# A new order for TensorE's steps in a slot of a fused attention kernel, with an aligned program stream

## Chip, cores and metric

The kernel runs on one core of one Trainium2 chip. The metric is device time in microseconds (us), the median of the runs; the kernel before takes 3887.73 us (3 runs, 3886.52 to 3889.18).

## What is computed

Input: 8 sequences of 512 tokens with 128 features, all in float32. An attention layer with a Taylor-series kernel comes first, then six layers of windowed attention with a feed-forward each, both wrapped in layer norms:

```python
x = x + _layernorm(_L0_attn_ref(_layernorm(x), ...))     # once, about the first 530 us
x = x + _layernorm(_L0_ffn_ref(_layernorm(x), ...))

def _L0_ffn_ref(x, ...):
    for i in range(DEPTH):                               # 6 layers
        x = attn_layer(shift_tokens(x), Wqkv[i], q_scale[i], k_scale[i], Wo[i]) + x
        x = ffn_layer(shift_tokens(x), ...) + x

def attn_layer(x, Wqkv, qs, ksc, Wo):                    # 16 heads of 64
    q, k, v = split(x @ Wqkv)
    q = l2norm(q) * qs ; k = l2norm(k) * ksc             # then rotary tables on q and k
    out = local_attention(q, k, v)                       # windows of 32, each sees itself and the one before
    return out @ Wo

def ffn_layer(x, ...):                                   # 128 -> 2 x 341 -> 128
    a, gate = split(layer_norm(x) @ W1 + b1)
    return a * gelu(gate) @ W2 + b2
```

## The kernel before

The change bears on the six layers. A *unit* is one block of 128 tokens of one sequence in one layer: 6 layers x 8 sequences x 4 blocks = 192 units. The main loop (L703) runs over *slots* t. In each slot TensorE does a different step for each of several units, so that the other engines have time between two steps of the same unit (`at(t, lag, step)` runs a step on unit t - lag):

- unit t: `proj` 0 and 1 (q and k, L421), `values` (v, L481), `unit_length` (the scaling of q and k);
- unit t-1: `by_features` 0 and 4 (transposes of q and k, four head pairs each, L511), `scores` (the mask L527, the scores L534, then maximum, exponentials and their sums);
- unit t-2: `by_keys` (transposes of the exponentials, L562), `weigh_values` (L574, the tile po), `out_by_features` (transposes of the result, L594);
- unit t-3: `out_project` (L603, the tile py, added to the state by VectorE at L608).

After the last block of a sequence the feed-forward follows, spread over slots: `feed_norm` with lag 3, `feed_first` 4, `feed_middle` 5 (gelu), `feed_last` 6. Each of these falls on one slot of four, so each slot has one of them.

TensorE's order is written out by hand (`tc.manual_schedule`, L694). The order of the instructions on VectorE, ScalarE and GpSimd is chosen by the framework's scheduler, from the order of the code, priorities (`tc.high_priority`) and extra edges that the kernel adds with `issue_behind`. SyncE issues the transfers, among them eight for each unit that spread v over the windows (L489 to L492).

The order of TensorE's steps in a slot is: q (`proj` 0), output projection, k (`proj` 1), transposes of exponentials, v (`values`), transposes of q and k (first half), po (`weigh_values`), transposes of q and k (second half), feed-forward step, mask and scores (tile sp), transposes of the result.

PSUM is divided into rings by tag. "mm" has two buffers of two banks: q, k, v and the feed-forward's products take turns. "tr" has two buffers of one bank: all transposes and py. "s" has one buffer of two banks: po and sp take turns. A step that takes a buffer waits until the readers of its last content are done.

What each product leaves for the other engines: q and k are read by VectorE (L429 twice, L436: the rotation) and by ScalarE (L444 twice: squares); their sums of squares are made at L457. v is copied by ScalarE (L482). Transposes are copied by ScalarE (L514 for q and k, L564 for the exponentials, L596 for the result). sp is read by the maximum (L542, VectorE) and the exponentials (L546, ScalarE, 16 instructions). po is divided by the sums at L582 (VectorE). The feed-forward's layer norm (L99 to L117) reads its PSUM tile nx twice, for the statistics (L105) and for the normalisation (L115).

## Time and profile before

| | |
|---|---|
| median of 3 runs | 3887.73 us |
| the profiled execution | 3893.85 us |
| its span (first to last instruction) | 3892.1 us |
| granted TensorE clock over the span | 0.99 |
| busy: TensorE, VectorE, ScalarE, GpSimd | 3729.8, 2818.2, 2657.5, 1837.0 us |
| TensorE's instructions | 65600 matmuls and as many weight loads |
| mean busy share of the DMA engines, 600 us to the end | 0.25 to 0.27 in each stretch |

The profile names an instruction by engine, line, operation and what it writes and reads: `sp<-kT,qT` is a matmul into the tile sp. PE is TensorE, PEld its weight loads, DVE VectorE, ACT ScalarE, POOL GpSimd. A float32 product shows as two matmuls for each one in the code. In a list of groups the numbers behind the bar are busy time, mean duration of one (ns) and the idle time of the engine just before; behind `<-` stands what ended it. In the list of waits a row gives who waited for whom, the total in us, how often, and the longest. "issue" is idle time with no releaser in the profile. In a timeline a row gives start, duration, engine and what ran; idle time before it stands in brackets. A matmul's end is modelled and reaches beyond the start of the next, so idle time between matmuls is a lower bound.

### The profile page before, as it was taken

The numbers are of one execution on the slowest core, as the hardware profiler recorded it, in microseconds if no ns is written. First come the engines' busy times: TensorE is split into PE (matmuls) and PEld (weight loads), VectorE is DVE, ScalarE is ACT, GpSimd is POOL, SyncE is SP. The second block draws the span as 40 slices with busy tenths as digits, with TensorE's granted clock in tenths as the row PEclk, the third lists the DMA queues.
The fourth block names the chain that finished last, engine by engine and source line by source line (L and its number), as shares of the span: only waits on it lengthen the run. The fifth ranks groups of instructions, "written<-read, shape, count | busy, mean of one in ns | idle before, by whom it ended". The sixth has DMA issues, their size and how long they took to land.

```text
span 3892.1 us, 149565 instructions
## 1 busy us (share of the span) xinstructions
PE 3729.8 (96%) x65600; PEld 2474.2 (64%) x65600; DVE 2818.2 (72%) x4300; ACT 2657.5 (68%) x6745; POOL 1837.0 (47%) x1311
## 2 busy tenths in 40 slices
PE   8999989999999999999999999999999999999997
PEld 4555456666666666666666666666666666666665
DVE  4555567777867777777777777777787777777775
ACT  5565656776767777777777677777677777766664
POOL 0000025555555555555555555555555555555552
PEclk9999999999999999999999999999999999999998
DMA  2000012222222222222222322223222222222221
GB/s 81 17 9 12 6 50 71 59 66 60 76 74 63 63 63 66 71 75 65 60 62 64 82 65 66 65 56 82 70 66 59 66 65 56 65 68 68 64 67 37
DMA packets 153208, 233.46 MB, mean 60 GB/s; under 512 B 32622, under 2 KB 53356, under 8 KB 151788
## 3 DMA queue, kind: packets, MB, share of 16 engines
q1 hardware_dynamic: 152556, 223.89, 22.4%
q8 instruction: 517, 8.47, 0.9%
q14 instruction: 135, 1.11, 0.1%
HBM read 24.54 MB, written 4.19 MB: 7 GB/s over the span
## 4 chain that ended last, share of the span: by engine, by line
PE 89%; ACT 5%; issue 3%; DVE 2%; DMA 0%; POOL 0%; POOLq 0%; DVEq 0%; SPq 0%; ACTq 0%
PE tr L70 17%; PE mm L421 17%; PE mm L481 9%; PE py L603 9%; PE sp L534 7%; PE po L574 6%; PE y L282 4%; PE mm L625 3%; PE py L657 3%; PE mm L626 3%; PE sc L252 2%; PE sp L527 2%; ACT sq L444 2%; PE vv L230 2%; PE po L318 2%
## 5 line engine op out<-in xcount | busy, mean ns | idle before, releaser
L454 POOL TENSOR_TENSOR qk<-t,t 128x1024 f32<-128x1024 f32 x384 | 909.2, 2368 | 999.6 <-DVE t L436 999.5
L421 PE MATMUL mm<-wqkv,state 128*128 128x512 f32 x1536 | 727.1, 596 | 3.7 <-ACT v L482 2.6
L470 POOL TENSOR_TENSOR qk<-qk,ss 128x1024 f32<-128x1024 f32 x384 | 722.3, 1902 | 16.0
L429 DVE TENSOR_TENSOR t<-mm,tab 128x512 f32<-128x512 f32 x768 | 497.8, 685 | 242.8 <-PE mm L421 231.3
L546 ACT ACTIVATE pe<-sp,mx 128x64 f32<-128x64 f32 x3072 | 651.4, 376 | 27.6 <-DVE mx L542 27.3
L436 DVE TENSOR_TENSOR t<-mm,tab 128x1024 f32<-128x1024 f32 x384 | 465.9, 1213 | 0.0
L457 DVE TENSOR_REDUCE ss<-sq 128x16 f32<-128x1024 f32 x384 | 461.9, 1203 | 2.0 <-ACT sq L444 2.0
L444 ACT ACTIVATE sq<-mm 128x512 f32<-128x512 f32 x768 | 422.6, 610 | 47.2 <-DVE t L436 45.6
L603 PEld LDWEIGHTS py<-oT,wo 128*128 128x128 f32 x3072 | 374.8, 193 | 93.5 <-issue 56.2
L70 PEld LDWEIGHTS tr<-ident,qk 128*128 128x128 f32 x3072 | 345.7, 141 | 127.1 <-issue 105.7
L70 PE MATMUL tr<-ident,qk 128*128 128x128 f32 x3072 | 412.1, 277 | 7.4 <-ACT qT L514 2.3
L596 ACT COPY oT<-tr 128x512 f32<-128x512 f32 x384 | 207.3, 589 | 266.2 <-PE tr L70 265.2
L421 PEld LDWEIGHTS mm<-wqkv,state 128*128 128x128 f32 x1536 | 264.1, 192 | 191.6 <-issue 188.0
L481 PE MATMUL mm<-wqkv,state 128*128 128x512 f32 x768 | 367.9, 602 | 16.8 <-ACT sq L444 16.8
L603 PE MATMUL py<-oT,wo 128*128 128x128 f32 x3072 | 376.0, 276 | 1.0 <-ACT oT L596 0.9
L582 DVE TENSOR_TENSOR on<-po,su 128x1024 f32<-128x1024 f32 x192 | 235.1, 1224 | 170.1 <-PE po L574 170.1
L534 PEld LDWEIGHTS sp<-kT,qT 64*32 64x32 f32 x24576 | 271.9, 106 | 116.7 <-issue 113.8
L574 PE MATMUL po<-v,pT 64*32 64x64 f32 x24576 | 299.3, 225 | 44.7 <-issue 44.7
L482 ACT COPY v<-mm 128x1024 f32<-128x1024 f32 x192 | 194.5, 1013 | 211.0 <-PE mm L481 211.0
L534 PE MATMUL sp<-kT,qT 64*32 64x64 f32 x24576 | 312.2, 227 | 26.0 <-issue 25.2
L574 PEld LDWEIGHTS po<-v,pT 64*32 64x32 f32 x24576 | 258.5, 105 | 86.4 <-issue 86.2
L542 DVE TENSOR_REDUCE mx<-sp 128x16 f32<-128x1024 f32 x192 | 234.6, 1222 | 106.9 <-PE sp L534 106.3
(108 smaller groups left out, 5171.0 us busy)
## 6 DMA issues: line engine op xcount, KB each, us to landing
v<-v SPq DMA_DIRECT2D x1152, 128.0 KB
v<-v SPq DMA_DIRECT2D x672, 64.0 KB
wqkv<-in_L_ffn_Wqkv_dram SPq DMA_DIRECT2D x6, 1536.0 KB
wo<-in_L_ffn_Wo_dram SPq DMA_DIRECT2D x6, 512.0 KB
xin<-_attn_hidden_states_dram SPq DMA_DIRECT2D x8, 256.0 KB
xr<-_attn_hidden_states_dram SPq DMA_DIRECT2D x8, 256.0 KB
x<-xr SPq DMA_DIRECT2D x8, 256.0 KB
xr<-x SPq DMA_DIRECT2D x8, 256.0 KB
```

The source lines that it names most:

```text
L70: nc.tensor.transpose(ps[:cols, :rows], src, ident[:rows, :rows])
L421: nc.tensor.matmul(ps[:, a].rearrange("p h d -> p (h d)"), lhs, wqkv[:, s, a, :], start=True, stop=True)
L429: nc.vector.tensor_tensor(t2[:, a], ps[:, 1 - a], tab[:, 2 * s + 1, j, HF * a : HF * (a + 1)].unsqueeze(1).to_broadcast([P, H, HF]), ALU.mult,
L436: nc.vector.tensor_tensor(t1, ps, tab[:, 2 * s, j, :].rearrange("p (a d) -> p a d", a=2).unsqueeze(2) .to_broadcast([P, 2, H, HF]), ALU.mult,)
L444: nc.scalar.activation(sq[:, :, a, :], ps[:, a], AF.Square)
L454: nc.gpsimd.tensor_tensor(qk[:, s].rearrange("p h a d -> p a h d"), t1, t2, ALU.add)
L470: nc.gpsimd.tensor_tensor(t, t, ss[:, i, :].unsqueeze(2).to_broadcast([P, H, HD]), ALU.mult)
L481: nc.tensor.matmul(ps[:, p, :], lhs, L["wqkv"][:, 2, p, :], start=True, stop=True)
L534: nc.tensor.matmul(sp[W * w : W * (w + 1), p, pair, :], qT[HD * p : HD * (p + 1), pair, W * w : W * (w + 1)], kT[HD * p : HD * (p + 1), pa ...
L546: ex = nc.scalar.activation(pe[:, pair, p, :], sp[:, p, pair, :], AF.Exp, bias=mx[:, p, pair : pair + 1])
L574: nc.tensor.matmul(po[W * w : W * (w + 1), p, pair, :], pT[r, pair, W * w : W * (w + 1)], v2[r, w, HD * pair : HD * (pair + 1)], start=Tru ...
L603: nc.tensor.matmul(py, L["wo"][:, c, :], oT[:, c, :], start=(c == 0), stop=(c == NP - 1))
```

## The change

1. **Order in a slot.** q, k, transposes of exponentials, output projection, first half of the transposes of q and k, po, second half of q's transposes, v, second half of k's, feed-forward step, mask and scores, transposes of the result.
2. **Rings.** py moves from "tr" to "s", so "s" is taken by py, po and sp in turn.
3. **v's copy.** `values` keeps the matmuls; the copy (L482) and the eight transfers become `spread`, called behind k's second transposes, the copy with an edge behind the last of the transposes' copies.
4. **Sums of squares.** Both are made behind the division of po.
5. **Mask.** For blocks other than a sequence's first, each of the two mask matmuls contracts over 32 rows with a new constant `each` (p = 0 on rows 0 to 31, p = 1 on rows 32 to 63) and no longer over 128 with the identity. `each` is built once, by eight VectorE copies.
6. **Norm.** The feed-forward's four normalisations become a step of their own, `feed_normed`, behind `scores`, with an edge behind the last maximum.
7. **Gelu's table** is loaded behind the copy of the transposed exponentials and no longer behind the last exponential.
8. **Alignment.** `addr_align(n, offset=o)` makes the loader put pad instructions into TensorE's program so that the next instruction lands o places past a multiple of n. Inside `feed_middle` each matmul but the first lands on a multiple of 16; in one slot of four (40 times) the instruction behind k's projection lands 98 places past a multiple of 128.

```diff
-        layer_norm(f2, xn, ps, NB, by_log=True)
+        u["normed"] = layer_norm(f2, xn, ps, NB, by_log=True, later=True)
+
+    def feed_normed(u):
+        u.pop("normed")(maxima[-1])
...
-        py = psum.tile([P, P], F32, tag="tr", name="py")
+        py = psum.tile([P, P], F32, tag="s", name="py", bufs=1)
...
-        mk = mask0 if u["j"] == 0 else mask
         sp = psum.tile([P, 2, NP, 2 * W], F32, tag="s", name="sp", bufs=1)
         for p in range(2):
+            r = slice(W * p, W * (p + 1))
+            lhs, mk = (identb, mask0) if u["j"] == 0 else (each[r], mask[r])
             nc.tensor.matmul(
-                sp[:, p], identb, mk.unsqueeze(1).to_broadcast([P, NP, 2 * W]),
+                sp[:, p], lhs, mk.unsqueeze(1).to_broadcast([lhs.shape[0], NP, 2 * W]),
                 start=True, stop=False, skip_group_check=True,
             )
...
-        nc.scalar.copy(v0, ps)
+        u["v0"], u["v0ps"] = v0, ps
+
+    def spread(u):
+        j, v0 = u["j"], u["v0"]
+        cp = nc.scalar.copy(v0, u.pop("v0ps"))
+        if copies:
+            issue_behind(cp, copies[-1])
...
         nc.tensor.matmul(pg[:cn, 0], w1[:, DI + c0 : DI + c0 + cn], xnT, start=True, stop=True)
+        nc.tensor.addr_align(FILL)
         nc.tensor.matmul(pg[:cn, 1], w1[:, c0 : c0 + cn], xnT, start=True, stop=True)
+        if c < NCH - 1:
+            nc.tensor.addr_align(FILL)
...
             gelus = 0 <= t - 5 < len(units) and units[t - 5]["j"] == NB - 1
+            at(t, 0, proj, 0)
+            at(t, 0, proj, 1)
+
+
+            if t % NB == 1 and NB < t <= len(units) - NB * (B - 1):
+                nc.tensor.addr_align(128, offset=IN_STEP)
+            at(t, 2, by_keys)
             if gelus:
                 gelu_only()
-            at(t, 0, proj, 0)
             at(t, 3, out_project)
-            at(t, 0, proj, 1)
-            at(t, 2, by_keys)
 
             if t == 0:
                 head_norm(NG - 1)
-            at(t, 0, values)
             if t == 1:
                 attn_out(B - 1)
+            at(t, 1, by_features, 0)
+            at(t, 2, weigh_values)
+            at(t, 1, by_features, 4, 0)
+            at(t, 0, values)
             if t == 3:
                 to_state(B - 1)
-            at(t, 1, by_features, 0)
-            at(t, 2, weigh_values)
+            at(t, 0, sum_squares, 0)
             at(t, 0, sum_squares, 1)
             if not gelus:
                 at(t, 0, unit_length)
-            at(t, 1, by_features, 4)
+            at(t, 1, by_features, 4, 1)
+            at(t, 0, spread)
             at(t, 3, feed_norm, ends=True)
             at(t, 4, feed_first, ends=True)
             at(t, 5, feed_middle, ends=True)
@@ -736,6 +773,7 @@
                 at(t, 0, unit_length)
             at(t, 6, feed_last, ends=True)
             at(t, 1, scores)
+            at(t, 3, feed_normed, ends=True)
             at(t, 2, out_by_features)
```

More of the change, by code (lines that the diff above doesn't have):

```diff
@@ L23 @@
 EPS = 1e-5
+FILL = 16
+IN_STEP = 98
 @with_exitstack
@@ L67, in sandwich_kernel @@
     mask0 = const.tile([P, 2 * W], BF16, tag="mask0", name="mask0")
+    each = const.tile([2 * W, P], BF16, tag="each", name="each")
+    for a in range(2):
+        for w in range(4):
+            nc.vector.tensor_copy(
+                each[W * a : W * (a + 1), W * w : W * (w + 1)], ident[W * a : W * (a + 1), W * a : W * (a + 1)]
+            )
     def transposed(ps, src, rows, cols):
         nc.tensor.transpose(ps[:cols, :rows], src, ident[:rows, :rows])
-    tables, exps, divisions = [], [], []
+    tables, exps, divisions, copies, pcopies, maxima = [], [], [], [], [], []
     def log_and_exp(behind):
@@ L82, in gelu_only @@
         ld = nc.scalar.preload_act_table_set("gelu_and_others")
-        issue_behind(ld, exps[-1])
+        issue_behind(ld, pcopies[-1])
         tables.append(ld)
@@ L97, in inverse_root, with layer_norm @@
         exps.append(nc.scalar.activation(dst, dst, AF.Exp, scale=-0.5))
-    def layer_norm(pool, dst, src, nb, by_log=False):
+    def layer_norm(pool, dst, src, nb, by_log=False, later=False):
         st = pool.tile([P, nb, 6], F32, tag="ln_st", name="ln_st")
@@ L113, in layer_norm, with last @@
             nc.vector.reciprocal(rs, rs)
-        for j in range(nb):
-            nc.vector.tensor_scalar(
-                dst[:, j, :], src[:, j, :], mv[:, j, 0:1], rs[:, j : j + 1], ALU.subtract, ALU.mult
-            )
+        def last(behind=None):
+            for j in range(nb):
+                t = nc.vector.tensor_scalar(
+                    dst[:, j, :], src[:, j, :], mv[:, j, 0:1], rs[:, j : j + 1], ALU.subtract, ALU.mult
+                )
+                if behind is not None:
+                    issue_behind(t, behind)
+        if later:
+            return last
+        last()
     psum = ctx.enter_context(tc.tile_pool(name="psum", bufs=2, space=PSUM))
@@ L450, in proj @@
         squared(1)
-        u["sq"] = sq
-        if s == 0:
-            sum_squares(u, 0)
+        u["sq", s] = sq
         nc.gpsimd.tensor_tensor(qk[:, s].rearrange("p h a d -> p a h d"), t1, t2, ALU.add)
@@ L457, in sum_squares @@
         su = nc.vector.tensor_reduce(
-            u["ss"][:, s], u["sq"].rearrange("p h a d -> p h (a d)"), AX.X, ALU.add
+            u["ss"][:, s], u["sq", s].rearrange("p h a d -> p h (a d)"), AX.X, ALU.add
         )
-        if s == 1 and divisions:
+        if divisions:
             issue_behind(su, divisions[-1])
@@ L496, in values, with by_features @@
         u["v2"] = v2
-    def by_features(u, c):
+    def by_features(u, c, which=(0, 1)):
         j, qk, B_ = u["j"], u["qk"], u["B"]
@@ L506, in by_features @@
             u["kT"] = B_["kT"]
-        for s in range(2):
+        for s in which if isinstance(which, tuple) else (which,):
             ps = psum.tile([P, 4, P], F32, tag="tr", name="tr")
@@ L513, in by_features @@
             with tc.high_priority():
-                nc.scalar.copy(dst, ps)
-        if c == NP - 4 and j < NB - 1:
+                copies.append(nc.scalar.copy(dst, ps))
+        if c == NP - 4 and s == 1 and j < NB - 1:
             B_["kT"] = f2.tile([P, NP, W + P], F32, tag="kT", name="kT")
@@ L541, in scores @@
         with tc.high_priority():
-            nc.vector.tensor_reduce(mx, sp, AX.X, ALU.max, negate=True)
+            maxima.append(nc.vector.tensor_reduce(mx, sp, AX.X, ALU.max, negate=True))
         pe = f2.tile([P, NP, 2, 2 * W], F32, tag="pe", name="pe")
@@ L563, in by_keys @@
             with tc.high_priority():
-                nc.scalar.copy(pT[:, c : c + 4, :], ps)
+                pcopies.append(nc.scalar.copy(pT[:, c : c + 4, :], ps))
     def weigh_values(u):
```

## The prediction

> **What bounds the kernel now.** I read the page's busy shares first, then the chain of work that ended last, then TensorE's waits, then its timeline slot by slot.

> ```profile
> PE 3729.8 (96%) x65600; PEld 2474.2 (64%) x65600; DVE 2818.2 (72%) x4300; ACT 2657.5 (68%) x6745; POOL 1837.0 (47%) x1311
> PE 89%; ACT 5%; issue 3%; DVE 2%; DMA 0%; POOL 0%; POOLq 0%; DVEq 0%; SPq 0%; ACTq 0%
> ```

> TensorE sets the end: it is busy 96% of the span and 89% of the chain. So only two things pay: fewer TensorE microseconds, or fewer waits of TensorE. The waits of TensorE, whole run:

> ```profile
> PE po L574 <- issue: 44.7, 62, 2.1
> PE sp L534 <- issue: 25.2, 25, 3.6
> PE mm L481 <- ACT sq L444: 16.8, 46, 2.2
> PE tr L70 <- ACT qT L514: 14.2, 48, 0.8
> PE tr L70 <- DVE fs L666: 13.6, 8, 1.7
> ```

> The first two have no releaser. They stand in the middle of the two steps made of tiny matmuls, each 256 instructions in 1.41 us (5.5 ns each):

> ```profile
> 2007.20 1.37 PE L574 MATMUL po<-v,pT 64*32 64x64 f32 x114
> 2009.19 0.34 PE L574 MATMUL po<-v,pT 64*32 64x64 f32 x14 [0.62 <-issue]
> ...
> 2010.90 0.59 PE L527 MATMUL sp<-mask,identb 128*128 128x512 bf16 x2
> 2011.42 1.21 PE L534 MATMUL sp<-kT,qT 64*32 64x64 f32 x100
> 2013.21 0.45 PE L534 MATMUL sp<-kT,qT 64*32 64x64 f32 x28 [0.58 <-issue]
> ```

> ```profile
> q8 instruction: 517, 8.47, 0.9%
> ```

> That queue carries TensorE's program: 8.47 MB in 517 packets of 16 KiB, that is 256 instructions of 64 bytes each. Numbering TensorE's recorded instructions (loads, matmuls, semaphore waits: 132,355), every idle stretch over 0.3 us that has no releaser falls at number 193 or 194 modulo 256; 76.8 of the 78.5 us of such idle time after 600 us lie there, none 128 further on. So they are waits for the next block of program, and they come when two block ends are passed close together (4.02 us apart above).

> Idle time alone understates a wait, because a matmul's recorded end reaches past its successor's start. So I took each step's time from its start to the next step's start, and subtracted the tenth percentile of that step. After 600 us TensorE loses 223 us: 132 us in steps that hold a block end (60 in po, 52 in sp, the rest spread), 91 us in others (19 by_keys ahead of values, 19 transposes of q and k ahead of the next transposes, 13 at a batch's end, the rest small).

> **The change, part by part** (192 slots; sums against this execution, 3893.85 us, span 3892.1; the median, 3887.73, is 6 us lower, and I take that off at the end).

> *Values no longer wait for the squares of q.* All three share the two mm buffers, so values needs q's released. Now 4.4 us lie between the end of q's projection and values (1.78 + 1.72 + 0.87); q's release takes 2.5 us of VectorE and 1.1 of ScalarE, and so it is late at times. Behind the change, k, weights, output projection, half the transposes, po and half of q lie between: 1.72 + 0.87 + 1.78 + 0.93 + 1.41 + 0.46 = 7.2 us. The wait goes: 18.7 lost in by_keys and 4.4 in values, -23 us. k's projection then reuses the buffer of the last values, copied out 1.6 us after k's transposes (0.6 for kT, 1.0 for v): mask, sp, transposes and q (4.3 us) cover it.

> *q, v, k apart.* The feed-forward's transposes no longer come right behind a q tile on its way out of PSUM; values lies between. -19 us.

> *Masks with 32 rows.* L527 costs 0.52 us a slot, two matmuls of 512 columns. In 144 slots the two now use different row groups. The attention's 32-row matmuls show what that gives:

> ```profile
> 483.73 1.14 PE L252 MATMUL sc<-tqk 32*128 32x512 f32 x8
> ```

> Eight passes in 1.08 us to the next step, against 0.43 each for a full one: over three times denser, four row groups at once. [...] I take 0.2 x 144: -29 us.

> *sp behind values.* From po's end to sp's start: 94 slots with 2.15 us lose 0.42 us each in sp, 46 with 4.3 us lose 0.21, 47 with 6.7 us lose 0. Values adds 1.72. Interpolated: 94 x 0.26 + 46 x 0.06 = 27 instead of 50: -23 us.

> *Aligned stream.* [...] Where the ends fall decides: 117 po stretches with the block end in their first 160 instructions lose nothing, 73 with it later lose 0.8 us each. A slot has 636 loads and matmuls plus about 6 semaphore waits, close to 5 x 128, so an end stands at one of two places 128 apart. Both places good: 0 us; one of them bad: 96 x 0.8 = 77; bad everywhere about 150. I take 38, the middle of the first two, against 60: -22. Other steps holding ends lose 20 now; I take 13: -7.

> *Padding* (up to 5 x 15 in a feed-forward, up to 127 in one slot of four, 40 times). No row shows a pad. From 0, if it is passed while queued wide matmuls run (3.4 us of q and k ahead of it), to 200 x 5.5 ns x 44 = 49 us. Wide matmuls stand ahead of every pad, so I take 0.

> *py in the s buffer.* New wait: po now needs both state additions on VectorE (0.57 us), and half the transposes (0.93 us) are all that covers them. Today they follow the multiplication that is running:

> ```profile
> 2054.07 1.21 DVE L436 TENSOR_TENSOR t<-mm,tab 128x1024 f32<-128x1024 f32 x1
> 2055.20 0.58 DVE L608 TENSOR_TENSOR state<-py,state 64x128 f32<-64x128 f32 x2
> ```

> The step behind py starts at 2054.38, so half the transposes would end at 2055.31; the additions ended at 2055.78, 0.47 late, since 0.65 us of the multiplication were left when py ended (2054.55). Directly behind py they would end at 2055.13, in time; behind k's whole rotation 0.5 to 0.6 late. Bounds 0 to 115 us, the row itself 90; but they are of high priority, and what runs when py ends is then a row of 0.6 or of 1.2 us at any point of it, so I take 0.1 a slot: +20. Queued behind po: transposes, values, sp. py itself waits for the exponentials of the scores before: they end about 4.9 us behind sp (1.2 maximum, 3.4 exponentials), py comes at 5.2. by_keys needs the first of them at 4.4: covered, by 0.2 to 0.5 us.

> *Norm behind the maximum.* The nx buffer now stays until maximum (1.2) and four normalisations (1.6) are done, 3.0 us behind sp; k's projection, its next user, comes 2.65 us behind sp.

> ```profile
> 2081.88 0.73 DVE L115 TENSOR_SCALAR xn<-nx,ln_mv,ln_rs 128x128 f32<-128x128 f32 x2 [0.60 <-ACT ln_rs L97]
> 2082.53 1.22 DVE L542 TENSOR_REDUCE mx<-sp 128x16 f32<-128x1024 f32 x1
> ```

> Here two of the four stand ahead of the maximum; that they no longer can shortens nothing on TensorE, which has transposes and projections to do. 48 x 0.3: +15 (0 to 25).

> *At nothing:* v's copy and its eight SyncE transfers come later, but their reader is two slots away; the gelu table (1.28 us) loads behind the copies of pT, 6 us ahead of gelu; both sums of squares behind the division end about 7 us ahead of need. If VectorE (13.9 us of work in a slot of about 16.5) slips, they share the fate of py.

> Sum: -23 - 19 - 29 - 23 - 22 - 7 + 0 + 20 + 15 = -88. 3893.85 - 88 = 3806 for the execution, 3800 against the median. Of the 223 us lost, some 40 are small waits behind copies that this sum leaves alone; a quarter of them should go with the longer distances, so I say **3790**.

> **Rivals.**
> (a) *Slower: po waits for the state additions.* If VectorE places k's rotation (2.5 us) and the sum over exponentials (1.2) ahead of them, po starts 1.2 us late in each slot: 192 x 1.2 = 230, so 3790 - 20 + 230 = 4000. It decides against the change from (98 + 20) / 192 = 0.61 us a slot. For it: VectorE is 72% busy, and fullest there. Against it: today they stand one instruction late, not more. Chance 0.17.
> (b) *The stream gains nothing:* the ends settle in the late part of po every other slot and the gap of 3.9 us ahead of sp is too short: +39 at po (77, not 38), +23 at sp, +15 of pads: 3867. Chance 0.2, a part of it within 0.2%.
> (c) *All goes as meant:* block waits fall to 15 us, no wait at po: 3790 - (78 - 15) - 20 = 3707, and 3690 if the norm costs nothing either. For it: 4 us between ends seems enough in the rows above. Chance 0.13.

> **How the numbers follow.** Forecast (3720 to 3850) 0.5, (b) 0.2, (c) 0.13, (a) 0.17. The range reaches down to (c) and up to (a) where it begins to decide: 3690 to 3900, leaving out most of (a) and the far part of (c). A measurement of this kernel can tell about 0.2% (8 us) from no change. Faster: 0.5 + 0.13 + 0.14 of (b) = 0.77; within: 0.06; slower: 0.17.

> **What would show it.** Right: in TensorE's waits the row of values behind sq and of the transposes behind qT gone; "issue" at po and sp below 45 us together; the two mask matmuls 0.3 us to sp's start; VectorE's additions ahead of po's start. Wrong: a row of po behind state L608, of k's projection (L421) behind the norm L115, of by_keys behind the exponentials, or issue waits at new lines as large as the old.

## The result and the profile after

The changed kernel takes 3829.34 us (median of 4 runs, 3824.57 to 3834.45) against 3887.12 for the kernel before: ratio 0.9852, 95% interval 0.9835 to 0.9869, 58 us less. Its profiled execution took 3825.62 us, 68.2 less than that of before.

The page's busy shares, chain by engine and program queue of the changed kernel:

```profile
PE 3703.6 (97%) x65600; PEld 2456.2 (64%) x65600; DVE 2794.7 (73%) x4308; ACT 2662.9 (70%) x6750; POOL 1842.6 (48%) x1311
PE 95%; issue 2%; ACT 2%; DVE 1%; POOL 0%; DMA 0%; POOLq 0%; SPq 0%; DVEq 0%; ACTq 0%
q8 instruction: 530, 8.68, 0.9%
```

TensorE now fills 95% of the chain. The program is 13 blocks longer (530 packets on q8 where there were 517, for 135,661 recorded instructions where there were 132,355), by 2936 pads and 370 more semaphore waits. From the list of TensorE's waits:

```profile
PE po L598 <- PE tr L79: 49.1, 189, 0.6
...
PE sp L558 <- issue: 6.4, 4, 2.1
PE po L598 <- issue: 6.1, 3, 2.0
```

The waits without a releaser fell from 44.7 and 25.2 us to 6.1 and 6.4. The rows of values behind the squares of q (16.8) and of the transposes behind qT (14.2) are down to 0.3 and 0.8. In their place there is one new row: po waits in 189 slots. The list names TensorE's own transposes as its releaser. The timelines of TensorE and of VectorE over the same microseconds say something else:

```profile
2009.57 1.95 PE L627 MATMUL py<-oT,wo 128*128 128x128 f32 x16
2011.36 1.04 PE L79 MATMUL tr<-ident,qk 128*128 128x128 f32 x8
2012.67 1.58 PE L598 MATMUL po<-v,pT 64*32 64x64 f32 x128 [0.28 <-PE tr L79]
```

```profile
2010.68 0.68 DVE L447 TENSOR_TENSOR t<-mm,tab 128x512 f32<-128x512 f32 x1
2011.28 0.24 DVE L577 RECIPROCAL su<-su 128x16 f32<-128x16 f32 x1
2011.44 0.63 DVE L447 TENSOR_TENSOR t<-mm,tab 128x512 f32<-128x512 f32 x1
2011.99 0.58 DVE L632 TENSOR_TENSOR state<-py,state 64x128 f32<-64x128 f32 x2
```

The state additions end at 2012.57, po starts at 2012.67. Over the slots po's start lies 100 to 102 ns behind them (5th to 95th percentile), while its distance from the start of the last transpose varies, 0.46 to 0.56 us. py ended at 2011.52; the additions started 0.47 us later, behind the second half of k's rotation (L447, in 187 of 190 slots).

Each step's time from its start to the next step's start, summed behind 560 us, shows where the microseconds went (from the traces):

| step | before | after | difference |
|---|---|---|---|
| transposes of q and k | 389.1 | 425.5 | +36.4 |
| po | 331.7 | 294.7 | -37.0 |
| mask | 101.2 | 70.4 | -30.8 |
| sp | 324.9 | 296.4 | -28.5 |
| by_keys | 194.8 | 179.4 | -15.4 |
| transposes of the result | 192.9 | 184.8 | -8.1 |
| q, k, v | 992.2 | 988.3 | -3.9 |
| feed-forward's first products | 253.6 | 264.6 | +11.0 |
| nx and xn | 50.9 | 59.3 | +8.4 |

A wait is booked here to the step ahead of it, so po's new wait stands in the first row. Of the losses in the last two rows, about 13.5 us belong to the new masks (see before_mask).

### The profile page after: what moved, and what is told of

It reads as the page before. It is cut to its first block, busy times and chain, and to the rows that moved or that the text cites. A ratio compares the mean times of both kernels' runs of the same rounds, so it can differ in the third digit from the quotient of the medians.

```text
span 3823.9 us, 152697 instructions
## 1 busy us (share of the span) xinstructions
PE 3703.6 (97%) x65600; PEld 2456.2 (64%) x65600; DVE 2794.7 (73%) x4308; ACT 2662.9 (70%) x6750; POOL 1842.6 (48%) x1311
## 4 chain that ended last, share of the span: by engine, by line
PE 95%; issue 2%; ACT 2%; DVE 1%; POOL 0%; DMA 0%; POOLq 0%; SPq 0%; DVEq 0%; ACTq 0%
PE tr L79 20%; PE mm L439 17%; PE py L627 9%; PE mm L497 9%; PE po L598 8%; PE sp L558 8%; PE y L300 4%; PE mm L652 3%; PE mm L654 3%; PE py L687 3%; PE sc L270 3%; PE sp L551 2%; PE vv L248 2%; PE qk L239 1%; PE po L336 1%
## 5 line engine op out<-in xcount | busy, mean ns | idle before, releaser
L439 PE MATMUL mm<-wqkv,state 128*128 128x512 f32 x1536 | 698.4, 597 | 2.6 <-ACT v L502 2.6
L447 DVE TENSOR_TENSOR t<-mm,tab 128x512 f32<-128x512 f32 x768 | 498.6, 671 | 239.5 <-PE mm L439 239.5
L439 PEld LDWEIGHTS mm<-wqkv,state 128*128 128x128 f32 x1536 | 273.7, 191 | 289.6 <-issue 242.2
L473 DVE TENSOR_REDUCE ss<-sq 128x16 f32<-128x1024 f32 x384 | 448.6, 1209 | 0.7 <-ACT sq L462 0.6
L79 PE MATMUL tr<-ident,qk 128*128 128x128 f32 x3072 | 440.7, 276 | 1.8 <-ACT qT L536 0.8
L536 ACT COPY kT<-tr 128x512 f32<-128x512 f32 x384 | 225.6, 587 | 299.6 <-PE tr L79 299.4
L627 PEld LDWEIGHTS py<-oT,wo 128*128 128x128 f32 x3072 | 364.5, 194 | 0.7 <-ACT oT L620 0.7
L497 PE MATMUL mm<-wqkv,state 128*128 128x512 f32 x768 | 363.1, 595 | 0.3 <-ACT sq L462 0.3
L598 PEld LDWEIGHTS po<-v,pT 64*32 64x32 f32 x24576 | 274.2, 105 | 98.0 <-PE tr L79 88.5
```

The costliest lines, as they stand in the source:

```text
L79: nc.tensor.transpose(ps[:cols, :rows], src, ident[:rows, :rows])
L439: nc.tensor.matmul(ps[:, a].rearrange("p h d -> p (h d)"), lhs, wqkv[:, s, a, :], start=True, stop=True)
L447: nc.vector.tensor_tensor(t2[:, a], ps[:, 1 - a], tab[:, 2 * s + 1, j, HF * a : HF * (a + 1)].unsqueeze(1).to_broadcast([P, H, HF]), ALU.mult,
L473: su = nc.vector.tensor_reduce(u["ss"][:, s], u["sq", s].rearrange("p h a d -> p h (a d)"), AX.X, ALU.add)
L497: nc.tensor.matmul(ps[:, p, :], lhs, L["wqkv"][:, 2, p, :], start=True, stop=True)
L598: nc.tensor.matmul(po[W * w : W * (w + 1), p, pair, :], pT[r, pair, W * w : W * (w + 1)], v2[r, w, HD * pair : HD * (pair + 1)], start=Tru ...
```

## The experiments

Each ratio is to the kernel before, run on the same chip; ratios from different chips are compared with each other. The kernel before takes 3889.2 us on two of the chips and 3901.9 on the third, where state_no_align, norm_first, values_early and state_all_aligned ran. Where those 13 us come from is not known, and a difference between chips can be off by as much. v's copy, the sums of squares and gelu's table (items 3, 4 and 7 of the change) were not tried alone.

**state_first**: the changed kernel, with VectorE's state additions ahead of the second half of k's rotation.

```diff
+        def rest():
+            second = turned(1)
+            if s == 1 and adds:
+                issue_behind(second, adds[-1])
+            straight()
...
             at(t, 3, out_project)
+            at(t, 0, rotate_rest)
```

> The changed kernel, with one edit: the second half of k's rotation, k's squares and the sum into qk are emitted behind the output projection, and the rotation's second half is put behind the state additions on VectorE. Theory A (po starts when VectorE's state additions are done, 0.10 us behind them in all 189 slots): the additions start at py's end and not 0.47 us later, po starts 0.38 us earlier in 189 slots, so about 70 us off: 3829 becomes 3760, ratio to the kernel before 0.967. Theory B (po waits for TensorE's own transposes, as the list of waits names it): no change, 3829, ratio 0.985.

Measured: 3756.48 us, ratio 0.9656 (0.9641 to 0.9672). Theory A. On VectorE and on TensorE:

```profile
1913.20 0.59 DVE L643 TENSOR_TENSOR state<-py,state 64x128 f32<-64x128 f32 x2
1913.83 0.69 DVE L447 TENSOR_TENSOR t<-mm,tab 128x512 f32<-128x512 f32 x1
```

```profile
1911.21 1.95 PE L638 MATMUL py<-oT,wo 128*128 128x128 f32 x16
1913.00 1.04 PE L79 MATMUL tr<-ident,qk 128*128 128x128 f32 x8
1913.97 1.51 PE L609 MATMUL po<-v,pT 64*32 64x64 f32 x128
```

The additions start at py's end (0.04 us behind it), and po starts 0.97 us behind the start of the transposes, not 1.31. The transposes' row falls from 425.5 to 364.8 us and that of po from 294.7 to 285.0: the 70 us that the change lost there. The releaser in the list of waits was the wrong one.

**no_align** (all `addr_align` taken out) and **offset_34**.

```diff
-        nc.tensor.addr_align(FILL)
...
-            if t % NB == 1 and NB < t <= len(units) - NB * (B - 1):
-                nc.tensor.addr_align(128, offset=IN_STEP)
```

```diff
-IN_STEP = 98
+IN_STEP = 34
```

> The changed kernel without any alignment (neither the multiples of 16 in the feed-forward nor the place in one slot of four). Theory A (the alignment keeps the ends of program blocks out of the bad places; the order alone does not): waits without a releaser return at po and sp, 40 to 90 us, 3870 to 3920, ratio 0.995 to 1.008. Theory B (the order alone ended them, because values now lies between po and sp; the pads cost 11 us in the feed-forward): 3815 to 3830, ratio 0.982 to 0.985.

> The changed kernel with the aligned place at 34 and not 98: block ends move by 64 instructions, in po from about 60 to 90 and 190 to 220 to about 0 to 30 and 125 to 155. Theory A (an end late in po is what costs, as before the change): the same or up to 15 us faster, ratio 0.981 to 0.985. Theory B (98 was a good place for reasons of sp or of the waits ahead of po): 20 us or more slower, ratio above 0.99.

Measured: no_align 3934.76 us, ratio 1.0123 (1.0103 to 1.0143); offset_34 3983.7 us, ratio 1.0244 (1.0226 to 1.0261). Without alignment the change is slower than the kernel before, by about 47 us; with the aligned place moved by 64 instructions, by about 95. no_align goes the way of its theory A but beyond its range; theory B of offset_34 held. TensorE's waits of no_align, then of offset_34:

```profile
PE po L598 <- issue: 49.6, 26, 2.6
PE po L598 <- PE tr L79: 47.0, 188, 0.6
PE tr L79 <- issue: 14.3, 10, 2.0
```

```profile
PE po L598 <- issue: 82.1, 40, 2.5
PE po L598 <- PE tr L79: 47.2, 187, 0.6
PE mm L497 <- issue: 29.5, 22, 1.9
```

The waits have no releaser, and nearly all stand at a block's end (numbers 193 and 194 modulo 256, as before). They are fewer and longer at po than before the change (26 of 1.9 us in the mean in no_align and 40 of 2.1 in offset_34, against 62 of 0.7). The program's own transfers fit: in all 207 waits over 0.3 us at a block's end in the traces of before, no_align and offset_34, the last packet of queue q8 landed 1.1 to 1.7 us before TensorE went on.

What makes an end costly? Counted from po's first matmul, 46 ends of offset_34 stand in po's last 16 instructions (241 to 255) and lose 2.2 us each in po; 23 stand in its first 16, and there TensorE waits 1.4 us just behind po (the row of L497); the other 123, at 16 to 167, cost 0.15 us or less on average. In the changed kernel 90 ends stand at 160 to 223 and cost 0.1 each. So "any end past 160", as read from the profile of before, was not the rule of the new order; the zone that costs is shorter and dearer.

The traces show what the costly places have in common. po passes 256 instructions in 1.4 us, so when one end falls late in po, the end before it was passed just ahead of po. In no_align 88 ends come less than 4 us behind the one before (the wait not counted): 48 of them wait, 75 of its 80 us. In offset_34 94 come within 3 us: 65 of them wait, 115 of its 122 us. The changed kernel has no end within 3 us of the last one, and 47 at 3 to 4 us, of which three wait, 6 us. In po a late place and a short distance are the same thing, so these runs do not separate the two. In the order of before the rule is weaker: ends within 4 us carry 40 of its 74 us; the others stand further apart, and why TensorE waits there these runs do not show.

**state_no_align**: state_first without any alignment.

> state_first without any alignment: what the order is worth by itself once po no longer waits for the state additions. Theory A (the two costs are independent): the 70 us of no_align go, 3935 becomes 3862, ratio 0.993; alignment is then worth 105 us here too. Theory B (the wait at po gave the fetching time, so that without it the waits for blocks grow): 3880 or more, ratio 0.998 or more.

Measured: ratio 0.9908 (0.9891 to 0.9925). Theory A: the two costs add. The step from no_align is 0.0215, or 84 us, where 70 were expected; it lies between two chips. The order with po's wait repaired is worth 0.9%, and alignment 2.5% on top of it (0.9656 against 0.9908).

**before_mask** (the kernel before with the 32-row masks) and **state_old_mask** (state_first with the old masks). The first takes over the change's `each` and its masks alone; the second goes the other way:

```diff
-            lhs, mk = (identb, mask0) if u["j"] == 0 else (each[r], mask[r])
+            lhs, mk = (identb, mask0) if u["j"] == 0 else (identb, mask)
```

> The kernel before with the 32-row mask matmuls alone. Theory A (two row groups work at once, and nothing waits for the time saved): 144 slots x 0.2 us = 29 us less, ratio 0.9925. Theory B (the time goes into the wait for a block of program, which then begins earlier): 0 to 15 us less, ratio 0.996 to 1.000.

> state_first with the two mask matmuls over 128 rows again, all else kept. Theory A (in an aligned stream the 32-row masks give the 29 us of the prediction): 3756 becomes 3785, ratio 0.973. Theory B (what before_mask shows holds here too: 30 us less in the mask, about 17 us more in the steps next to it): 3765 to 3770, ratio 0.968 to 0.969.

Measured: before_mask 3882.22 us, ratio 0.9984 (0.9975 to 0.9992), 7 us; state_old_mask 3775.11 us, ratio 0.9704 (0.9690 to 0.9717) beside 0.9649 for state_first run again on that chip: 21 us. The masks' own step falls by 30 us in before_mask, as computed. But the steps next to it grow: nx +3.4, xn +4.5, the feed-forward's products +5.5, sp +5 and the transposes of the result +3. Waits over 0.3 us without a releaser hardly change (74 us behind 600 us before, 71 in before_mask), so theory B of before_mask named the wrong place. One slot with xn, in the kernel before and in before_mask:

```profile
2026.06 0.66 PE L70 MATMUL tr<-ident,xn 128*128 128x128 f32 x4 [0.25 <-ACT qT L514]
2026.56 0.59 PE L527 MATMUL sp<-mask,identb 128*128 128x512 bf16 x2
2027.08 1.82 PE L534 MATMUL sp<-kT,qT 64*32 64x64 f32 x128
```

```profile
2025.79 0.66 PE L77 MATMUL tr<-ident,xn 128*128 128x128 f32 x4 [0.35 <-ACT qT L521]
2026.37 0.39 PE L535 MATMUL sp<-mask,each 32*128 32x512 bf16 x2
2026.69 1.77 PE L542 MATMUL sp<-kT,qT 64*32 64x64 f32 x128
```

The mask takes 0.32 us and not 0.52, but xn takes 0.58 and not 0.50: 0.12 are left of the 0.20. The records of all slots show the same, from the start of one matmul to the start of the next. The last matmul of nx and of xn takes 205 ns ahead of a 32-row mask, against 109 to 127 ahead of a 128-row one, and the last of the feed-forward's products 525 against 429. With the old masks put back (state_old_mask) it is 109 and 429 again, and ahead of the masks of a sequence's first block, which stay at 128 rows, nothing changes (428). The same cost stands ahead of po in the kernel before (202 against 109) and between mask and sp: 306 ns with the old masks and 315 with the new, against 215 for a mask that another follows. So in these traces each of these passages, from 128 rows to 64 or 32 and from the 32 rows of the new masks to the 64 of sp, costs about 0.1 us. The old masks have one such passage, at sp; the new ones have two. What is left of the gain is 0.203 - 0.096 us in 144 slots, 15 us by this estimate, between the 7 and the 21 that were measured.

**norm_first**: the four normalisations ahead of the scores again, without the edge.

```diff
-        u.pop("normed")(maxima[-1])
+        u.pop("normed")()
...
             at(t, 3, feed_norm, ends=True)
+            at(t, 3, feed_normed, ends=True)
...
             at(t, 1, scores)
-            at(t, 3, feed_normed, ends=True)
```

> The changed kernel with the four normalisations ahead of the scores and without the edge behind the maximum, as before the change. Theory A (the prediction: the nx buffer is then free earlier, k's projection no longer waits, 15 us): 3815, ratio 0.981. Theory B (k's projection does not wait, its step costs the same as before the change; but the maximum stands behind a normalisation again, and the transposes of the exponentials wait): 3829 to 3850, ratio 0.985 to 0.990.

Measured: ratio 0.9941 (0.9925 to 0.9958), beside 0.9852 for the change: 35 us slower by the ratios. Theory B, and above its range. VectorE, ScalarE and TensorE of norm_first in one such slot:

```profile
1992.50 1.37 DVE L127 TENSOR_SCALAR xn<-nx,ln_mv,ln_rs 128x128 f32<-128x128 f32 x4 [0.60 <-ACT ln_rs L106]
1993.78 1.22 DVE L566 TENSOR_REDUCE mx<-sp 128x16 f32<-128x1024 f32 x1
```

```profile
1995.03 3.39 ACT L570 ACTIVATE pe<-sp,mx 128x64 f32<-128x64 f32 x16 [1.12 <-DVE mx L566]
```

```profile
1993.08 3.60 PE L439 MATMUL mm<-wqkv,state 128*128 128x512 f32 x8
1996.51 2.29 PE L79 MATMUL tr<-ident,pe 128*128 128x128 f32 x8
```

sp ended at about 1992.3; the maximum starts 1.5 us later, behind the normalisations, and the exponentials end at 1998.4. by_keys, which the new order runs already at 1996.5, is stretched with them: 2.14 us in the 47 slots with a norm, against 0.87 in the changed kernel. That is 60 us by the traces; why the ratios show 35 is open, but the two ran on different chips.

**values_early**: v's projection ahead of po again.

```diff
+            at(t, 0, values)
             at(t, 2, weigh_values)
             at(t, 1, by_features, 4, 0)
-            at(t, 0, values)
```

> The changed kernel with v's projection ahead of po, as before the change; its copy stays behind k's transposes. VectorE's state additions then have 1.72 us more cover, so the wait of po goes (-70 us). Between po and sp 1.72 us are missing. Theory A (the distance between the two dense steps decides what a block end costs): sp loses 0.4 us or more a slot again, +75 or more, so 3830 to 3950, ratio 0.985 to 1.016. Theory B (the aligned places are enough by themselves): 3760 to 3775, ratio 0.967 to 0.971.

Measured: ratio 0.9903 (0.9888 to 0.9918). The ratio lies within theory A, but it came about in another way than I wrote. po's wait is gone (the transposes' row is 365.8), sp loses 28.5 us (324.9 against 296.4) and not 75, and a new wait comes:

```profile
PE mm L439 <- DVE xn L127: 32.5, 46, 1.1
PE sp L558 <- issue: 22.8, 32, 3.6
```

k's projection waits for the normalisations to leave nx: the wait that the prediction expected of the change itself. In the changed kernel v's projection lies between po and nx, and VectorE is through with the division and both sums of squares when nx comes: in one such slot it starts on the statistics of nx 0.3 us behind nx's end, in values_early 2.0 us.

**state_all_aligned** (state_first with the aligned place in all sequences but the first) and **state_late** (the same, without the multiples of 16 in the last layer's feed-forward).

```diff
-            if t % NB == 1 and NB < t <= len(units) - NB * (B - 1):
+            if t % NB == 1 and NB < t <= len(units):
```

```diff
-        nc.tensor.addr_align(FILL)
+        if l < DEPTH - 1:
+            nc.tensor.addr_align(FILL)
```

> state_first, with the aligned place kept in the last seven sequences too (47 times, not 40). state_first has 11.7 us of waits for program blocks behind 3250 us, where the alignment stops, and almost none ahead of it. Theory A: they go, 3756 becomes about 3745, ratio to the kernel before 0.963. Theory B (the last layer's slots hold extra transposes, and the fixed place is no better there): no change, 0.966.

> state_first, aligned in the last seven sequences too, but without the pads of 16 in the last layer's feed-forward, so that the aligned place there needs about 45 pads and not 122. A pad takes about 76 ns (35 of them 2.65 us), q and k in the queue hide 3.4 us. Theory A (pads cost what the queue does not hide): 45 x 0.076 = 3.4 us, hidden or nearly; the 12 us of block waits behind 3250 us go, 3745, ratio 0.963. Theory B (the last layer costs the same however it is aligned): 0.966 or more.

Measured: state_all_aligned ratio 0.9693 (0.9679 to 0.9707), slower than state_first. state_late 3744.93 us, ratio 0.9629 (0.9615 to 0.9642), beside state_first again:

> state_first once more, as the base for the two other kernels on the same chip. Ratio to the kernel before 0.966 as before, between 0.964 and 0.967.

Measured 3754.74 us, ratio 0.9649 (0.9632 to 0.9666). The intervals of the two overlap, so state_late's 10 us are likely rather than certain; they match the 12 expected, and its trace behind 600 us has no wait over 0.3 us without a releaser, where that of state_first has 11.7 us. In state_all_aligned neither po nor sp waits for a block any more; what it has instead, TensorE's longest wait and one of its five places:

```profile
PE tr L79 <- issue: 26.8, 5, 5.5
```

```profile
3349.48 2.74 PE L439 MATMUL mm<-wqkv,state 128*128 128x512 f32 x6
3357.73 1.94 PE L79 MATMUL tr<-ident,pe 128*128 128x128 f32 x8 [5.51 <-issue]
```

The five places stand behind 122 pads each, which take 9.5 to 9.9 us; 5.4 us of that in the mean stand as TensorE's wait (26.8 in five), and the rest passes while matmuls of q and k run. In all but two of the 40 places of the changed kernel 10 pads are enough, 0.7 us, and TensorE has no idle time behind them.

## Why the prediction was right, and where its sum was off

The forecast was 3790 us within 3690 to 3900; 3829 was measured. The direction and most of the mechanisms held; the sum of -88 us became -68 in the profiled execution. That it came so close is in part luck: py cost 50 us more than forecast, and alignment, the norm and sp gave 36 more back. And the range held because the aligned place is a good one, which the prediction did not know: at 34 instead of 98 the same change takes 3984 us, outside it.

- **Values behind q's squares**: -23 forecast; by_keys and v fell by 20.
- **q, v, k apart**: -19 forecast. The loss was in the 47 slots in which the feed-forward's transposes used to follow: the second half of the transposes of q and k took 64.2 us there, and 43 to 45 in each other kind of slot. That excess of 20 us is gone. In state_first, where no new wait hides it, the whole row fell by 24.
- **Masks**: -29 forecast; the step itself 31, the kernel 7 to 21 (before_mask, state_old_mask). The 0.2 us a slot in the sum was my estimate, and no row of the kernel before shows it for a pair; in the trace of the changed kernel the second 32-row mask starts 3 ns behind the first, where a 128-row one starts 216 ns behind (both medians). The forecast took the saving of one step for that of the path: the two masks are 0.203 us shorter, but the step ahead of them is 0.096 us longer.
- **sp behind values**: -23 forecast; -28.5 measured, and the same 28.5 back in values_early. The sum was right, but not the interpolation by distance. The 98 slots with the short distance lost 0.4 us each and now lose 0.01 at 3.5 us, where 0.16 was forecast (-40 us in sum); the slots with 5.8 and 8.4 us lose 0.2, where 0.15 and nothing was forecast, and that is more than before.
- **Aligned stream**: -22 at po and -7 elsewhere forecast; -37 at po and -8 in the transposes of the result measured. The reading that close ends cost was right for this order, but the price was not: 0.8 us for any end past 160, and 77 us for one bad place of two. no_align and offset_34 lose 105 and 154 us against the change. The count of 636 instructions in a slot also leaves out the feed-forward's 8 to 24, and most ends spread over 40 places in each half of po (48 to 87, 176 to 215). Few ends hold the time: in no_align 435 of 487 ends behind 600 us pass without a wait, and the other 52 hold the 80 us.
- **Padding**: 0 forecast, nearly right: the feed-forward's products take 264.6 us with the pads and 260.5 without (no_align). The bound of 5.5 ns a pad was wrong. In the trace of the changed kernel a pad takes about 76 ns (35 of them 2.65 us).
- **py in the s buffer**: +20 forecast, +70 measured. This is the term that was furthest off. Its own row said 0.47 us a slot, or 90 us; I argued it down to 0.1 by priority. The additions again stood behind the rest of an instruction and started 0.47 us after py; po lost 0.37 us in 189 slots. Rival (a) is the same mechanism; its point of decision, 0.61 us a slot, was not reached.
- **Norm behind the maximum**: +15 forecast at k's projection; there it cost nothing. What I put at nothing is its gain: without it by_keys waits, and the change loses 35 us or more. I judged the move by what by_keys waits for in the old order, where output projection and k stood ahead of it.

Rival (b) says that the stream gains nothing; with the alignment left out this happens, and then the change is slower, not 20 us faster. state_late meets both conditions of rival (c), no wait at po and under 15 us of waits for blocks, and takes 3745 us where (c) said 3707.

## What to carry to other kernels

When a step is moved earlier, go through what it reads again: a wait that had slack in the old order (here maximum, exponentials and their transposes) can become the next bound. Where a row of the trace prices a new wait, take that price; here the state additions, of high priority, still started 0.47 us behind py, after what already ran on VectorE. A matmul that becomes cheaper by using fewer rows can make the step ahead of it longer (here 0.203 us less at the masks and 0.096 more ahead of them): read both steps. And look for idle time without a releaser at equal distances in the instruction count (here every 256: 44.7 us at po and 25.2 at sp before the change), and at how soon one block's end follows the last, before you judge an order. Here the same order was 1.5% faster and 2.4% slower at two places of the stream.
